# Attention and two quantised convolutions on one core: ScalarE and VectorE in the order of the source, and a Winograd combination in three pieces

## The chip, the cores and the metric

The kernel runs on one core of a Trainium2 chip. The metric is the device time of one execution in microseconds, the median of the runs. The engines are TensorE (PE, matmul), VectorE (DVE), ScalarE (ACT), GpSimd (POOL) and SyncE (SP, which issues DMAs).

## The reference

The input x has 16 images of 128 channels by 32 x 32 pixels, float32. Two layers follow each other:

```
# layer 0: attention over the 1024 pixels of each image, 4 heads of 128 channels
q, k, v = split(w_qkv . x + b_qkv)
out = softmax(q k^T / sqrt(128)) v           # per image and head
x1 = w_out . out + b_out + x
# layer 1: two 3x3 convolutions with 4-bit activations and weights, batch norms
a = round(clip(x1, 0, 1) * 15) / 15
y = batchnorm(conv3x3(a, quantised(w1)))
z = batchnorm(conv3x3(round(clip(y, 0, 1) * 15) / 15, quantised(w2)))
result = z + x1
```

The batch norms take mean and variance over all 16 images, so the second convolution can't begin before the first one is done for the last image.

## The kernel before

**Steps.** The work lies in `fast_path`. The attention has 64 heads (16 images x 4); each but the last takes NK = 4 steps, k = 0 to 3, and the last one has a form of its own (`score_unit`, `attend_unit`). A step does, in the order of the source:

1. `scores(g, k)`: four score products on TensorE into `pss` (512 wide, pool `ps_s`, three PSUM buffers), each followed by an exponential on ScalarE (L556) into a slice of the tile `e` (pool with two buffers). VectorE then makes the combinations that a Strassen-like product needs: T3 (L559), T1 and T2 (L560), T4 (L563), and adds the row sums into `es` (L567 at k=1, which reads the `e` of k=0 and of k=1; L569 at k=2 and 3).
2. `run(step, 0)`: what the table `later` holds for the first half of the step.
3. `attend(g, k-1)`: seven products of `e` and `vo` into the four banks `psa` (one buffer each). The last product of a head (k=3) goes to bank 0.
4. `run(step, 1)`: what `later` holds for the second half.

**What `later` holds.** The loop over heads fills it with `at(step, half, function)`; entries of one key keep the order in which they were added, and head g's are added before head g+1's. For a head that ends at step `end`: `sum_up` 0 (row sums, `part`, L630) at `end`, first half; `evacuate` (four copies of `psa` to SBUF on ScalarE, L600) at `end`, second half; `combine` 0, 1, 2 (L610 to L623: copies on ScalarE, adds on VectorE) at `end`+1 to `end`+3; `sum_up` 1 to 3 (L649 to L662); `normalise` (L679 to L694) at `end`+3, second half, whose last operation releases the image. `project_u` for the next head and `project_v` for the next image (vo, L535 to L538) lie between these.

**The first convolution** is spread over the attention too. After every second image (an image pair p) its inputs are quantised (`quantize`, L260 to L262) at `end`+5, and a Winograd form of the convolution runs in small pieces through the next six heads: `six_columns` (L827 to L842) and `six_rows` (L853) on VectorE, `six_products` (psw on TensorE, a copy on ScalarE at L862, then VectorE at L884 to L904), in three parts s = 0, 1, 2. `first_statistics` ends the pair at `end`+24. Image 14 has a smaller form (`products`), the last image a plain convolution.

**What sets the order.** On TensorE every product is chained to the one before it (`product` with `tc.issue_after`), so that it keeps the order of the source. `tc.issue_after(ins)` lets what is traced within it come after `ins` on its engine, with no wait added. ScalarE and VectorE have no such chain in the attention: the planner orders their instructions, by the order of the source among those that are ready by its own estimates of time. SyncE issues the writes of x1 (L696) and of the finished first-convolution outputs of eight images (L955); ScalarE's queue issues the loads of x (L423), each of which needs the buffer of an image two earlier.

The lines that set the order of the evacuation and of attend's last product:

```
for to, ps in zip(evs[g], psa.pop(g)):          # evacuate, banks 0, 1, 2, 3
    nc.scalar.copy(to, ps)
...
if k % 2:                                       # attend, (bank, half, value, exponential)
    seven = [seven[i] for i in (1, 0, 3, 2, 5, 4)] + [(0, 1, S3, T3)]
```

Of the kernel before, what the change touches and what calls it, by code (L numbers as in the profile page):

```python
# [192 lines left out]
def fast_path(  # L193
# [29 lines left out]

    outer = ExitStack()
# [28 lines left out]
    def quantize(b, src, scale, bias, r0=0, r1=H):  # L253

        cut = slice(r0 * W, r1 * W)
        t = qtp.tile([P, (r1 - r0) * W], F32, tag="qt", name="qt")
        if b == B - 1 and scale == A_LEVELS and r1 == H:
            nc.vector.tensor_scalar(t, src[:, cut], scale, 0.0, ALU.mult, ALU.max)
        else:
            nc.scalar.activation(t, src[:, cut], AF.Relu, bias=bias, scale=scale)  # L260
        nc.vector.tensor_scalar(t, t, A_LEVELS, MAGIC, ALU.min, ALU.add)
        return nc.vector.tensor_scalar(  # L262
            pads[b % NPAD][:, r0 + 1 : r1 + 1, 1 : W + 1],
            t.rearrange("p (h w) -> p h w", w=W),
            MAGIC,
            None,
            ALU.subtract,
        )
# [82 lines left out]
    def sums_range(b):  # L351
        flat = sums[:, b * NH : (b + 1) * NH, :].rearrange("p g k -> p (g k)")
        nc.vector.tensor_reduce(ext[:, 0, b : b + 1], flat, AX.X, ALU.min)
        nc.vector.tensor_reduce(ext[:, 1, b : b + 1], flat, AX.X, ALU.max)
# [23 lines left out]
    with ExitStack() as ph:  # L378
# [86 lines left out]
        def fold_a(h):  # L465
# [10 lines left out]
            nc.vector.tensor_scalar(at_sb[:, h, :], ps[:, 0:P], qscale, None, ALU.mult)  # L476
            nc.vector.tensor_scalar(au_sb[:, h : h + 1], bias, qscale, None, ALU.mult)

        def fold_b():
# [3 lines left out]
            nc.scalar.copy(bt_sb[:, 1, 1:], ps)  # L483
            nc.vector.tensor_copy(bt_sb[:, 1, 0], ps[:, NH - 1])
            nc.scalar.copy(bt_sb[:, 0, :, TOP], bt_sb[:, 1, :, TOP])  # L485
            nc.vector.tensor_tensor(
                bt_sb[:, 0, 0:NH, BOTTOM], bt_sb[:, 1, 0:NH, BOTTOM], bt_sb[:, 1, 0:NH, TOP], ALU.subtract
            )
            nc.vector.tensor_copy(bt_sb[:, 0, NH, BOTTOM], bt_sb[:, 1, NH, BOTTOM])

        def fold_bo():
# [9 lines left out]
            nc.vector.tensor_tensor(bo2_sb, ps, bo_sb, ALU.add)  # L501

        def project_u(g, hf, ps=None):
# [7 lines left out]
            if g == 0 and hf == 0:  # L511
                nc.vector.tensor_scalar(dst, ps, au_sb[:, h : h + 1], None, ALU.add)
            else:
                copied = nc.scalar.activation(dst, ps, AF.Identity, bias=au_sb[:, h : h + 1])  # L514
                if g == 0:
                    load_rest(copied.ins)
# [8 lines left out]
        def project_v(b, k, c, ps=None):  # L525
# [9 lines left out]
            nc.scalar.copy(v[:, c : c + 3 : 2], ps.rearrange("p (h a o) -> p a h o", a=2, o=PH))  # L535
            if c == 1:
                nc.vector.tensor_tensor(v[:, S2], v[:, S3], v[:, A22], ALU.subtract)
                nc.vector.tensor_tensor(  # L538
# [9 lines left out]
        def scores(g, k, between=None):  # L548
# [4 lines left out]
            for i, (c, m) in enumerate(((0, 1), (1, 1), (0, 0), (1, 0))):  # L553
                ps = ps_s.tile([P, HALF], F32, tag="s", name=f"pss_{g}_{k}_{i}")
                score(ps, b, g, k + NK * c, ts(m, HALF))
                exps[:] = [nc.scalar.activation(e[:, 2 * c + 1 - m], ps, AF.Exp).ins]  # L556
                if between and i in between:
                    between[i]()
            nc.vector.tensor_tensor(e[:, T3], e[:, B12], e[:, B22], ALU.add)  # L559
            nc.vector.tensor_tensor(  # L560
                e[:, T1 : T2 + 1 : T2 - T1], e[:, B12 : B11 + 1], e[:, B11 : T3 + 1 : T3 - B11], ALU.subtract
            )
            nc.vector.tensor_tensor(e[:, T4], e[:, T2], e[:, B21], ALU.add)  # L563
            mine = e[:, T4 : T3 + 1]
            if k == 1:
                sides[g] = esp.tile([P, NHF, HALF], F32, tag="es", name=f"es_{g}")
                nc.vector.tensor_tensor(sides[g], es[g, 0][:, T4 : T3 + 1], mine, ALU.add)  # L567
            elif k > 1:
                added = nc.vector.tensor_tensor(sides[g], sides[g], mine, ALU.add)  # L569
                sums_added[:] = [added.ins]  # L570
# [26 lines left out]
        def evacuate(g):  # L597
            evs[g] = [evp.tile([P, HALF], F32, tag=f"s{i}", name=f"ev_{g}_{i}") for i in range(4)]
            for to, ps in zip(evs[g], psa.pop(g)):
                nc.scalar.copy(to, ps)  # L600
# [5 lines left out]
        def combine(g, part):  # L606
            sa, sb, s3, sd = evs[g]
            if part == 0:
                y = avs[g, "y"] = evp.tile([P, HALF], F32, tag="y", name=f"y_{g}")
                nc.scalar.copy(y[TOP], s3[BOTTOM])  # L610
                nc.scalar.copy(y[BOTTOM], sd[TOP])  # L611
                nc.scalar.copy(sd[TOP], sd[BOTTOM])
                nc.vector.tensor_tensor(y, sa, y, ALU.add)  # L613
                return
            y = avs[g, "y"]
            if part == 1:
                nc.scalar.copy(s3[BOTTOM], y[TOP])
                nc.vector.tensor_tensor(y, y, s3, ALU.add)
            elif part == 2:
                nc.scalar.copy(sa[BOTTOM], y[BOTTOM])  # L620
                avs[g] = avp.tile([P, N], F32, tag="av", name=f"av_{g}")
                nc.vector.tensor_tensor(avs[g][:, HALF:], y, sd, ALU.add)
                nc.vector.tensor_tensor(avs[g][:, 0:HALF], sa, sb, ALU.add)  # L623
                evs.pop(g), avs.pop((g, "y"))

        def quadrant_sums(total):
# [3 lines left out]
            nc.vector.tensor_reduce(  # L630
# [8 lines left out]
        def sum_up(g, part):  # L639
# [5 lines left out]
            elif part == 1:  # L645

                side = smp.tile([Q, P // Q, n], F32, tag="side", name=f"side_{g}")
                for a in range(P // Q):
                    nc.scalar.copy(side[:, a, :], sides[g][ts(a, Q), :])  # L649
                sides[g] = side  # L650
            elif part == 2:
                total = smp.tile([Q, n], F32, tag="total", name=f"total_{g}")
                nc.vector.tensor_reduce(
# [4 lines left out]
                nc.vector.tensor_tensor(first, first, second, ALU.add)  # L658
                nc.vector.reciprocal(rinv[0:Q, :], total)
            else:  # L660
                for a in range(1, P // Q):
                    nc.scalar.copy(rinv[ts(a, Q), :], rinv[0:Q, :])  # L662

        def last_sums(part, cut):
# [7 lines left out]
            nc.vector.reciprocal(rinv, ps)  # L672

        def spread(g, cut):
# [4 lines left out]
            nc.vector.transpose(rb, rinv.unsqueeze(2).to_broadcast([P, rinv.shape[1], Q]))  # L679
            return rb  # L680

        def normalise(g):
# [3 lines left out]
            if h == 0:  # L686
                accs[b] = accp.tile([P, N], F32, tag="acc", name=f"acc_{b}")
                nc.vector.tensor_tensor(accs[b], av, rb, ALU.mult)
                return
            nc.vector.tensor_tensor(av, av, rb, ALU.mult)  # L690
            nc.vector.tensor_tensor(accs[b], accs[b], av, ALU.add)
            if h == NH - 1 or g == LAST - 1:

                nc.vector.scalar_tensor_tensor(accs[b], accs[b], bo2_sb, xt[b], ALU.add, ALU.add)  # L694
# [15 lines left out]
        def score_unit(u):  # L710
# [9 lines left out]
            exps[:] = [nc.scalar.activation(e, ps, AF.Exp).ins]  # L720

        def attend_unit(u):
# [8 lines left out]
            elif u == FIRST_UNIT[i] + 1:  # L731
# [6 lines left out]
                nc.vector.tensor_tensor(totals[i], units[(u - 1) // 4][:, (u - 1) % 4], e, ALU.add)  # L738
            else:
                nc.vector.tensor_tensor(total, total, e, ALU.add)  # L740
# [15 lines left out]
            elif u + 1 == FIRST_UNIT[i + 1]:  # L756
# [3 lines left out]
                nc.scalar.copy(avs[LAST, i], psa[LAST, i])  # L760
                sides[LAST, i] = quadrant_sums(total)

        def normalise_group(i):
# [5 lines left out]
            nc.vector.tensor_tensor(rb, avs.pop((LAST, i)), rb, ALU.mult)  # L769
            nc.vector.tensor_tensor(x1[:, cut], x1[:, cut], rb, ALU.add)  # L770
# [14 lines left out]
        def transform_weights():  # L785
            with tc.issue_after(sums_added[0]):
                by_row = once.tile([P, 4, 3, P], BF16, tag="rows", name="wino_rows")
                w = wq[0].rearrange("p (y x) o -> p y x o", x=3)
                nc.vector.tensor_copy(by_row[:, 0], w[:, 0])
                nc.vector.tensor_copy(by_row[:, 1], w[:, 2])  # L790
                nc.vector.tensor_tensor(by_row[:, 3], w[:, 0], w[:, 2], ALU.add)
                nc.vector.tensor_tensor(by_row[:, 2], by_row[:, 3], w[:, 1], ALU.add)
                nc.vector.tensor_tensor(by_row[:, 3], by_row[:, 3], w[:, 1], ALU.subtract)
                nc.vector.tensor_scalar(by_row[:, 2:4], by_row[:, 2:4], 0.5, None, ALU.mult)
                left, mid, right = [by_row[:, :, x, :] for x in range(3)]
                nc.vector.tensor_copy(wino[:, 0], left)
                nc.vector.tensor_copy(wino[:, 5], right)
                nc.vector.tensor_tensor(wino[:, 4], left, right, ALU.add)
                nc.vector.tensor_tensor(wino[:, 1], wino[:, 4], mid, ALU.add)
                nc.vector.tensor_tensor(wino[:, 2], wino[:, 4], mid, ALU.subtract)  # L800
                nc.vector.scalar_tensor_tensor(wino[:, 4], right, 4.0, left, ALU.mult, ALU.add)
                nc.vector.scalar_tensor_tensor(wino[:, 3], mid, 2.0, wino[:, 4], ALU.mult, ALU.add)
                nc.vector.scalar_tensor_tensor(wino[:, 4], mid, -2.0, wino[:, 4], ALU.mult, ALU.add)
                flat = wq[0].rearrange("p t o -> p (t o)")
                nc.vector.tensor_scalar(flat, flat, FIRST, None, ALU.mult)
# [11 lines left out]
        def six_columns(p, s, g):  # L817
# [8 lines left out]
            if s == 0:  # L826
                nc.vector.tensor_tensor(t, at(1), at(2), add)  # L827
                nc.vector.tensor_tensor(u, at(3), at(4), add)
                nc.vector.scalar_tensor_tensor(one, t, -4.0, u, mult, add)
                nc.vector.tensor_tensor(t, at(1), at(2), sub)  # L830
                nc.vector.tensor_tensor(u, at(4), at(3), sub)
                nc.vector.scalar_tensor_tensor(two, t, 4.0, u, mult, add)
            elif s == 1:
                nc.vector.tensor_tensor(t, at(3), at(1), sub)
                nc.vector.tensor_tensor(u, at(4), at(2), sub)
                nc.vector.scalar_tensor_tensor(one, t, 2.0, u, mult, add)
                nc.vector.scalar_tensor_tensor(two, t, -2.0, u, mult, add)
            else:
                nc.vector.scalar_tensor_tensor(t, at(2), -5.0, at(4), mult, add)
                nc.vector.scalar_tensor_tensor(one, at(0), 4.0, t, mult, add)  # L840
                nc.vector.scalar_tensor_tensor(u, at(3), -5.0, at(5), mult, add)
                nc.vector.scalar_tensor_tensor(two, at(1), 4.0, u, mult, add)  # L842

        def six_rows(p, s, i):
# [6 lines left out]
            for k, (x, y, op) in enumerate(OF_FOUR):  # L851
                into = tiles[p][:, i, k].rearrange("p (g i j) -> p g i j", g=2, j=D4)
                nc.vector.tensor_tensor(into, pick(x), pick(y), op)  # L853

        def two_products(name, weights, operands, scale, k):
# [6 lines left out]
            nc.scalar.mul(ms[name][:, k : k + 2], ps, scale)  # L862
# [5 lines left out]
        def six_products(p, s, i, k):  # L868
# [15 lines left out]
            nc.vector.tensor_tensor(e, two, of(2).unsqueeze(1).to_broadcast(list(two.shape)), ALU.add)  # L884
            nc.vector.tensor_tensor(e[:, 0], e[:, 0], of(3), ALU.add)
            nc.vector.tensor_tensor(e[:, 1], e[:, 1], of(3), ALU.subtract)
# [6 lines left out]
            if s == 2:  # L893
                y = y[3 * i]
                nc.vector.tensor_tensor(y, y, other if i else one, ALU.add)
# [629 lines left out]
```

## Time and profile before

| what | value |
|---|---|
| runs | 2093.58 and 2095.42 us, median 2094.5 |
| the profiled execution | 2096.73 us |
| its span | 2094.9 us, granted TensorE clock 0.987 |
| TensorE busy (matmul) | 2014.9 us, 96% |
| VectorE busy | 1796.4 us, 86% |
| ScalarE busy | 1278.9 us, 61% |
| GpSimd busy | 19.6 us, 1% |

The span runs from the first to the last instruction. In the lines of the profile, a group or an instruction is named by line, engine, operation, output and input; a number in square brackets with an arrow is the idle time of the engine just before it and what ended that. In the timeline the first two columns are start and duration in microseconds, and x4 means four instructions merged into one row. Ends of matmuls are modelled. The attention fills the time to about 2000 us; the second convolution and the end take the rest.

### The profile page before, as it was taken

What the parts mean: (1) busy time and instruction counts of PE and PEld (TensorE: products, weight loads), DVE (VectorE), ACT (ScalarE), POOL (GpSimd) and SP (SyncE); (2) the same over time, 40 slices, a digit from 0 to 9 for tenths busy, and PEclk for the clock granted to TensorE, in tenths of its full rate; (3) what the DMA queues carried; (4) which work ended last, traced back from release to release, by engine and by line L of the source; (5) the groups of instructions that cost most, each with busy time, mean ns of one, the idle gap of its engine ahead of it and who ended that gap; (6) DMA issues with size and microseconds to landing.
All of it is one profiled execution on the core that took longest, in us unless ns stands there. A gap on an engine that the chain in (4) does not pass through costs nothing.

```text
span 2094.9 us, 25194 instructions
## 1 busy us (share of the span) xinstructions
PE 2014.9 (96%) x9505; PEld 890.8 (43%) x9505; DVE 1796.4 (86%) x2692; ACT 1278.9 (61%) x2480; POOL 19.6 (1%) x29
## 2 busy tenths in 40 slices
PE   8999999999999999999999999999999999999994
PEld 3443434443353434534345343444345343453452
DVE  4878788897988988898888988989789888889998
ACT  4565566566566666656656656656665665665575
POOL 0000000000000000000000000000000000000020
PEclk9999999999999999999999999999999999999997
DMA  1000000000000000000000000000000000000064
GB/s 40 23 1 21 1 21 1 20 1 1 21 1 21 1 21 1 1 21 1 21 1 20 21 1 20 1 21 21 1 21 1 21 21 21 1 1 11 21 251 162
DMA packets 13329, 45.86 MB, mean 22 GB/s; under 512 B 1424, under 2 KB 1808, under 8 KB 13200
## 3 DMA queue, kind: packets, MB, share of 16 engines
q1 hardware_dynamic: 10000, 34.15, 4.3%
q10 hardware_dynamic: 3200, 10.03, 1.5%
q8 instruction: 76, 1.25, 0.2%
q14 instruction: 53, 0.43, 0.1%
HBM read 23.21 MB, written 20.97 MB: 21 GB/s over the span
## 4 chain that ended last, share of the span: by engine, by line
PE 64%; DVE 24%; ACT 8%; issue 3%; DMA 0%; POOL 0%; DVEq 0%; ACTq 0%
PE pss L408 27%; PE psa L408 26%; DVE e L560 4%; PE psv L408 4%; PE psu L408 4%; ACT e L556 3%; DVE es L569 2%; DVE e L563 2%; ACT ev L600 2%; DVE part L630 2%; DVE e L559 1%; DVE es L567 1%; PE psc L287 1%; ACT side L649 1%; DVE av L690 1%
## 5 line engine op out<-in xcount | busy, mean ns | idle before, releaser
L408 PE MATMUL pss<-u,x 128*64 128x512 f32 (+1 forms) x4128 | 1061.0, 592 | 25.8 <-ACT e L556 23.2
L408 PE MATMUL psa<-e,vo 128*64 128x512 f32 (+1 forms) x3624 | 934.6, 595 | 19.3 <-DVE e L563 19.3
L556 ACT ACTIVATE e<-pss 128x512 f32<-128x512 f32 x1008 | 579.9, 594 | 308.3 <-PE pss L408 258.6
L408 PEld LDWEIGHTS pss<-u,x 128*64 128x64 f32 x4128 | 405.5, 137 | 500.6 <-issue 343.1
L408 PEld LDWEIGHTS psa<-e,vo 128*64 128x64 f32 x3624 | 363.4, 138 | 463.7 <-issue 375.0
L560 DVE TENSOR_TENSOR e<-e 128x1024 f32<-128x1024 f32 x252 | 307.2, 1219 | 26.3 <-ACT e L556 23.7
L559 DVE TENSOR_TENSOR e<-e 128x512 f32<-128x512 f32 x252 | 172.2, 683 | 86.0 <-ACT e L556 85.3
L563 DVE TENSOR_TENSOR e<-e 128x512 f32<-128x512 f32 x252 | 172.4, 684 | 10.1 <-DVE e L560 0.9
L408 PE MATMUL psv<-bt_sb,x 128*64 128x512 f32 x512 | 179.7, 593 | 1.0 <-ACT bt_sb L485 1.0
L408 PE MATMUL psu<-x,at_sb 128*64 128x512 f32 x512 | 174.7, 604 | 2.3 <-ACT wino L862 1.5
L649 ACT COPY side<-part 32x32 f32<-32x32 f32 x252 | 54.5, 216 | 179.1 <-DVE part L630 176.6
L600 ACT COPY ev<-psa 128x512 f32<-128x512 f32 x252 | 137.9, 586 | 42.3 <-PE psa L408 40.4
L569 DVE TENSOR_TENSOR es<-es,e 128x1024 f32<-128x1024 f32 x126 | 153.8, 1220 | 1.9
L535 ACT COPY vo<-psv 128x512 f32<-128x512 f32 x128 | 75.0, 586 | 80.8 <-PE psv L408 80.7
L514 ACT ACTIVATE u<-psu,au_sb 128x512 f32<-128x512 f32 x127 | 87.3, 687 | 22.7 <-PE psu L408 21.0
L862 ACT ACTIVATE wino<-psw 128x512 f32<-128x512 f32 x92 | 55.0, 598 | 70.5 <-PE psw L408 69.3
L679 DVE STREAM_TRANSPOSE rb<-sums 128x1024 f32<-128x1024 f32 (+1 forms) x66 | 79.6, 1207 | 12.0 <-ACT sums L662 11.9
L613 DVE TENSOR_TENSOR y<-ev,y 128x512 f32<-128x512 f32 x63 | 43.3, 688 | 52.8 <-ACT y L611 52.8
L408 PEld LDWEIGHTS psv<-bt_sb,x 128*64 128x64 f32 x512 | 58.7, 137 | 61.3 <-issue 49.2
L408 PEld LDWEIGHTS psu<-x,at_sb 128*64 128x64 f32 x512 | 54.4, 139 | 65.8 <-issue 52.4
L630 DVE TRANSPOSE_TENSOR_REDUCE part<-es 128x32 f32<-128x1024 f32 (+1 forms) x65 | 79.6, 1224 | 0.6
L567 DVE TENSOR_TENSOR es<-e,e 128x1024 f32<-128x1024 f32 x63 | 76.8, 1219 | 0.3
(198 smaller groups left out, 1435.4 us busy)
## 6 DMA issues: line engine op xcount, KB each, us to landing
x_dram<-acc SPq DMA_DIRECT2D x16, 512.0 KB, 4.3
x<-in_x_dram ACTq DMA_DIRECT2D x15, 512.0 KB, 4.6
res<-x_dram SPq DMA_DIRECT2D x1, 7680.0 KB, 32.4
y_dram<-y SPq DMA_DIRECT2D x4, 1024.0 KB, 4.0
back<-y_dram SPq DMA_DIRECT2D x1, 4096.0 KB, 14.1
out_dram<-back SPq DMA_DIRECT2D x8, 512.0 KB, 4.3
out_dram<-y SPq DMA_DIRECT2D x9, 256.0 KB, 2.4
out_dram<-y SPq DMA_DIRECT2D x3, 512.0 KB, 5.0
```

The lines of the kernel that those rows point to most:

```text
L408: done = nc.tensor.matmul(out_, lhsT=lhsT, rhs=rhs, start=start, stop=stop)
L514: copied = nc.scalar.activation(dst, ps, AF.Identity, bias=au_sb[:, h : h + 1])
L556: exps[:] = [nc.scalar.activation(e[:, 2 * c + 1 - m], ps, AF.Exp).ins]
L559: nc.vector.tensor_tensor(e[:, T3], e[:, B12], e[:, B22], ALU.add)
L560: nc.vector.tensor_tensor(e[:, T1 : T2 + 1 : T2 - T1], e[:, B12 : B11 + 1], e[:, B11 : T3 + 1 : T3 - B11], ALU.subtract)
L563: nc.vector.tensor_tensor(e[:, T4], e[:, T2], e[:, B21], ALU.add)
L567: nc.vector.tensor_tensor(sides[g], es[g, 0][:, T4 : T3 + 1], mine, ALU.add)
L569: added = nc.vector.tensor_tensor(sides[g], sides[g], mine, ALU.add)
L600: nc.scalar.copy(to, ps)
L630: nc.vector.tensor_reduce(part, total.rearrange("p (k c) -> p k c", c=Q), AX.X, ALU.add, apply_transpose=True,)
L649: nc.scalar.copy(side[:, a, :], sides[g][ts(a, Q), :])
L679: nc.vector.transpose(rb, rinv.unsqueeze(2).to_broadcast([P, rinv.shape[1], Q]))
```

## The change

A small class hands every call to an engine and chains it behind the last instruction that it handed out. Through it go all ScalarE and VectorE computations of the attention and of the first convolution within it: `quantize`, `sums_range`, `fold_a`, `fold_b`, `fold_bo`, `project_u`, `project_v`, `scores`, `evacuate`, `combine`, `sum_up`, `last_sums`, `spread`, `normalise`, `score_unit`, `attend_unit`, `normalise_group`, `transform_weights`, the Winograd functions. Not through it go the DMAs that ScalarE issues, `conv_weights`, `constants`, `bn_constants`, `statistics`, `gather`, the plain convolutions and all that follows the attention.

The second edit takes four operations on the pair's outputs (L901 to L904) out of `six_products` (where they ran with the last piece of part s=1, at `end`+18, second half) and makes of them a function `six_mix`, called in two halves at `end`+20.

```diff
+    class InOrder:
+        def __init__(self, engine):
+            self.engine, self.last = engine, None
+        def __getattr__(self, name):
+            def call(*args, **kwargs):
+                with tc.issue_after(self.last) if self.last else nullcontext():
+                    done = getattr(self.engine, name)(*args, **kwargs)
+                self.last = done.ins
+                return done
+            return call
+
+    act, vec = InOrder(nc.scalar), InOrder(nc.vector)
...
             for to, ps in zip(evs[g], psa.pop(g)):
-                nc.scalar.copy(to, ps)
+                act.copy(to, ps)
...
             elif i == 1:
                 sums, differences = (y[0], y[1]) if s == 0 else (y[2], y[3])
-                nc.vector.tensor_tensor(sums, one, other, ALU.add)
-                nc.vector.tensor_tensor(differences, one, other, ALU.subtract)
-                if s == 1:
-                    nc.vector.tensor_tensor(y[0], y[0], y[2], ALU.add)
-                    nc.vector.scalar_tensor_tensor(y[2], y[2], 3.0, y[0], ALU.mult, ALU.add)
-                    nc.vector.scalar_tensor_tensor(y[1], y[3], 2.0, y[1], ALU.mult, ALU.add)
-                    nc.vector.scalar_tensor_tensor(y[3], y[3], 6.0, y[1], ALU.mult, ALU.add)
+                vec.tensor_tensor(sums, one, other, ALU.add)
+                vec.tensor_tensor(differences, one, other, ALU.subtract)
+
+        def six_mix(p, n):
+            y = [
+                y2[p].rearrange("p g (i j c) -> p (g i) j c", j=D4, c=4)[..., c] for c in (n, n + 2)
+            ]
+            if n == 0:
+                vec.tensor_tensor(y[0], y[0], y[1], ALU.add)
+                vec.scalar_tensor_tensor(y[1], y[1], 3.0, y[0], ALU.mult, ALU.add)
+            else:
+                vec.scalar_tensor_tensor(y[0], y[1], 2.0, y[0], ALU.mult, ALU.add)
+                vec.scalar_tensor_tensor(y[1], y[1], 6.0, y[0], ALU.mult, ALU.add)
...
+                    for n in range(2):
+                        at(end + 20, n, six_mix, p, n)
                     at(end + 24, 0, first_statistics, b)
```

## The prediction

> **What bounds the kernel now.** I read the page first, then the matrix multiplies' gaps in the timeline, then the chain behind those gaps, then the lists of waits.
>
> ```profile
> PE 2014.9 (96%) x9505; PEld 890.8 (43%) x9505; DVE 1796.4 (86%) x2692; ACT 1278.9 (61%) x2480; POOL 19.6 (1%) x29
> ...
> PE   8999999999999999999999999999999999999994
> ```
>
> TensorE is nearly full in every slice, so the change can gain only what its gaps hold. An image pair of the attention (32 steps) recurs every 247.2 us: the x_dram writes of every second image start at 1026.16, 1273.89 and 1521.11 us. In such a pair TensorE shows these gaps over 0.25 us (timeline of PE, cut at the gaps):
>
> ```profile
> 1410.24 4.71 PE L408 MATMUL psa<-e,vo 128*64 128x512 f32 x13 [2.71 <-DVE e L563]
> ...
> 1426.24 1.08 PE L408 MATMUL pss<-u,x 128*64 128x512 f32 x4 [0.55 <-ACT e L556]
> ...
> 1468.55 1.08 PE L408 MATMUL pss<-u,x 128*64 128x512 f32 x4 [0.30 <-ACT e L556]
> ...
> 1539.39 1.08 PE L408 MATMUL pss<-u,x 128*64 128x512 f32 x4 [1.60 <-ACT e L556]
> ```
>
> That is 5.2 us per pair. The same list from 98 us to 1954 us sums to 42 us, 2% of the time. The 2.71 is the combination of the pair: six y operations run on VectorE in a block, and the exponentials' sums wait behind it (timeline of DVE, one pair later):
>
> ```profile
> 1648.58 1.10 DVE L898 TENSOR_TENSOR y<-six 128x512 f32<-128x512 f32 x1
> 1649.52 1.11 DVE L899 TENSOR_TENSOR y<-six 128x512 f32<-128x512 f32 x1
> 1650.46 1.15 DVE L901 TENSOR_TENSOR y<-y 128x512 f32<-128x512 f32 x1
> ...
> 1654.56 0.67 DVE L559 TENSOR_TENSOR e<-e 128x512 f32<-128x512 f32 x1
> ```
>
> The planner does not keep the source order today. ScalarE starts evacuating a finished head before its last product is done, because the banks finish one by one:
>
> ```profile
> 1225.03 0.58 ACT L600 COPY ev<-psa 128x512 f32<-128x512 f32 x1
> 1225.87 0.58 ACT L600 COPY ev<-psa 128x512 f32<-128x512 f32 x1 [0.26 <-PE psa L408]
> 1226.73 1.07 ACT L600 COPY ev<-psa 128x512 f32<-128x512 f32 x2 [0.27 <-PE psa L408]
> ```
>
> The head's last psa matmul starts only at 1226.10 and ends at 1226.69. The same trace also shows what happens when all four copies come late and in one block (ACT, then PE):
>
> ```profile
> 1289.57 2.05 ACT L600 COPY ev<-psa 128x512 f32<-128x512 f32 x4
> 1291.48 0.64 ACT L556 ACTIVATE e<-pss 128x512 f32<-128x512 f32 x1
> ```
> ```profile
> 1292.18 1.08 PE L408 MATMUL pss<-u,x 128*64 128x512 f32 x4 [1.61 <-ACT e L556]
> ```
>
> The first exponential of the next step is delayed, and the fourth score, which needs that PSUM buffer (ps_s has three), starts 0.06 us after it ends.
>
> Last, the step that has no filler on VectorE shows what the order of the source costs there:
>
> ```profile
> 1308.23 1.23 DVE L560 TENSOR_TENSOR e<-e 128x1024 f32<-128x1024 f32 x1 [0.17 <-ACT e L556]
> 1309.56 0.69 DVE L563 TENSOR_TENSOR e<-e 128x512 f32<-128x512 f32 x1
> 1310.29 1.23 DVE L569 TENSOR_TENSOR es<-es,e 128x1024 f32<-128x1024 f32 x1
> 1311.55 1.25 DVE L630 TRANSPOSE_TENSOR_REDUCE part<-es 128x32 f32<-128x1024 f32 x1
> ```
>
> An operation that reads its predecessor's result starts 1.33 us (1024 wide) or 0.73 us (512 wide) after it. Independent neighbours follow after 1.14 and 0.60 us (1650.46 after 1649.52 is likewise 0.94 for 1.11). Today the planner puts independent work between the dependent ones.
>
> **The Trainium skill.** "PSUM — Partial Sum Buffer", section Engine vs sequencer instructions: ScalarE's and VectorE's queues are strict FIFO and matmuls complete in program order. The trace agrees: at 1289.57 exponentials stand behind copies. "Perfetto Trace Analysis", section Optimizing Tensor Performance: independent groups rotate through banks so that one's evacuation overlaps the next one's matmuls; at 1225.03 it does. "VectorE: DVE Perf Modes", section The DRAIN you can't avoid: the next operation waits until the pipe is empty. The trace shows this only for dependent neighbours; independent ones overlap by 0.08 us, and I use the trace.
>
> **Part 1: the pair's combination in pieces.** Four operations of about 1.02 us move from step 18 after the pair's end to steps 20 (two, half 0) and 20 (two, half 1). No operation is added and no DMA moves; SP's and POOL's queues are not passed. The two sums and differences (L898, L899) stay. This frees the 2.7 us gap, 7 times, but puts 4.4 us (dependent order) into step 20, where the old image's last normalisation already lags.
>
> **Part 2: ScalarE in source order.** evacuate copies the banks in the order 0, 1, 2, 3, and bank 0 gets the head's very last product (k=3 is odd: S3, T3). So none of the four can start before the end of the last product. Let E be the time at which TensorE can issue the next matmul. The last matmul ends at about E+0.38, the first copy starts at E+0.42, copies follow each other by 0.48 (1289.57 to 1291.48 for four), the exponential starts at E+2.34 and ends at E+2.92, and the fourth score starts at E+2.98. Three scores cover 3 x 0.86 = 2.58. The stall is 0.40 us at a plain head. Where a value projection comes ahead of the copies in the list (head 0 of each image), the copies wait for its psv: stall 0.88. Where a psw product comes ahead (steps 8 and 20): 0.68. Where the projection follows the copies (head 3): its 0.86 us of matmuls hide it. A pair has two of 0.88, 0.68, 0.40 and 0 each: 3.9 us. Seven pairs give 27, and the first 8 heads (no psw) 2.5: 30 us. Behind the waiting copy stand the exponentials, and TensorE waits for these.
>
> **Part 3: VectorE in source order.** I tally its work per step against TensorE's length. A step is 16 score and 14 attend matmuls at 0.215 = 6.45 us, plus 0.86 for each u or v projection, 0.43 for a psw, all stretched by 1.2% (clock 0.987). VectorE's e operations in order: 0.73+1.33+0.73+1.14 = 3.93 (2.66 at k=0, which has no es). To this come, in dependent order: part 1.15 (k=0); y 0.6 (k=1); y and total 1.55 (k=2); two av adds 1.2 and normalise 2.44, 3.7 or 5.04 (k=3; heads 0, 1-2, 3); vo 1.1; quantize 1.3; six_columns 2.35, 1.5 or 1.6 per image; six_rows 0.85; six_products with k=2 1.4, plus 1.98 or 1.1 for y. The exponentials alone hold es to 6.96 us after a step's start. The sums that matter (steps after the pair's end; us from the step's start):
>
> ```
> step  PE    queue free  es done  all done   lag into next
>  3    6.5      1.1        7.0      13.2        6.7
>  5    7.8      4.4        8.3      12.5        4.7
>  7    7.0      6.0       10.0      14.4        7.5
>  8    7.4      7.5       10.1      15.7        8.3
>  9    8.5      8.3       12.2      16.2        7.7
> 12    8.3      8.5       11.2      16.7        8.4
> 13    7.8      8.4       12.3      12.9        5.1
> 19    6.5      4.1        8.0      16.0        9.4
> 20    7.0      9.4       12.1      18.0       11.1
> 21    8.6     11.1       15.0      19.4       10.8
> ```
>
> Most of the lag is hidden: e is needed a step later, after the next scores. The tight place is k=1. There es (L567) is the last reader of the e buffer of k=0 (the pool has two), and the next step's exponentials need this buffer; the fourth score needs the first of them. Stall = es done + 0.7 - (step + 2.6): step 9 1.8 us, step 13 2.5, step 21 4.5, steps 20 to 25 another 1.1. Together 9.9 us per pair, 69 for seven. In the trace of before this wait exists ("ACT e L556 <- DVE es L567", 25.9 us in 30 times, longest 1.8), but it never reached TensorE for long.
>
> This tally is sensitive: with all VectorE work 5% shorter it gives 3.6 us per pair, with 10% 1.6, with 5% more 17. The trace has no stage in strict order to fix it; below nothing is excluded, since lag absorbs all. I take the middle.
>
> **Sum.** Against the profiled execution (2096.7 us; its span 2094.9, 1.8 around it): +30 + 69 - 38 (the gaps listed, less the last two near 1951, which belong to the last images) = +61, so 2157.7. The runs' median is 2.2 lower: 2155.5, say 2156. The stage after the attention is not touched except through the first convolution's quantize: 0.
>
> **The rivals.**
> - A: only the copies cost. VectorE's lag stays inside the buffers because the work is some 10% less than tallied. Speaks for it: VectorE has 14% idle. Against: dependent neighbours lose their overlap 96 times a pair in the e operations alone. 30 + 11 - 38 = +3: 2098.
> - B, not slower: the order itself pays. Today bulk work is put ahead of e operations by wrong due times; in source order e comes first and all gaps over 0.25 us go. The place is the head change: it decides if the copies are done early enough that the first exponential ends within 2.58 us of E, for which the first copy would have to start before E+0.02. For: the 2.71 gap is such a mistake. Against: bank 0 is last. -38: 2057.
> - C: on top of the forecast, the load of x (L423) is not in the chain, and is queued on ScalarE by the planner's times. At step 20 its releaser (L694) ends near 9.4 us, while the copies could go at 7.4: 2 us on seven pairs, +14: 2170.
>
> **How the numbers follow.** Forecast 0.60, A 0.18, B 0.10, C 0.12. The range runs from A (2098, a little below it) to the tally with 5% more work and C's part, 2094.5 + 17 x 7 + 30 - 38 + 14 = 2220: 2096 to 2222. The same sum with 5% less work gives 2112. Two per cent, about what a measurement of this kernel can tell from no change, is 42 us: slower means above 2136. Of the forecast some five sixths lie above (0.50), nearly all of C (0.11): slower 0.61. B reaches faster only if the smaller gaps go as well: 0.03. Same 0.36.
>
> **What would show it.** In the profile of after, the copies at L600 should come as x4 of about 2.0 us after the last psa, PE gaps of 0.4 to 0.9 "<-ACT e L556" at head changes, a long gap near step 21 with "ACT e L556 <- DVE es L567" far above 25.9 us, and no 2.7 us psa gap near step 18. "ACT side L649 <- DVE part L630" (176.6 us today) should shrink, as side copies stand behind exponentials. Wrong: if L567 stays below 30 us in total (then A), or if the copies still start before the head's last product ends (then the part on ScalarE falls), or if psa waits on L563 grow most (then the e buffers are not the tight place).

## The result and the profile after

The changed kernel takes 2179.5 us (2178.4 to 2180.6) against 2094.5 us before: a ratio of 1.041, interval 1.036 to 1.045. The forecast was 2156 in 2096 to 2222. The profiled execution's span is 2176.6 us, 81.7 more than before, at a granted clock of 0.979. All chained instructions now carry the line of the helper, L233, and TensorE's products L425, so the page is read by tiles.

The page's busy line and TensorE's slices:

```profile
PE 2041.7 (94%) x9505; PEld 857.9 (39%) x9505; DVE 1856.0 (85%) x2692; ACT 1286.5 (59%) x2480; POOL 20.3 (1%) x29
...
PE   9999998999998999999999999999999899998984
```

No engine became the bound over the whole span: VectorE's busy time grows by 60 us at the same count of instructions, but its share falls by a point. The time lies in TensorE's gaps. One image pair of the timeline of PE, cut at gaps over 0.25 us (as before, the last bracket is idle time and its releaser):

```profile
1301.30 1.08 PE L425 MATMUL pss<-u,x 128*64 128x512 f32 x4 [0.56 <-ACT e L233]
1330.64 1.08 PE L425 MATMUL pss<-u,x 128*64 128x512 f32 x4 [0.36 <-ACT e L233]
1359.64 1.08 PE L425 MATMUL pss<-u,x 128*64 128x512 f32 x4 [0.56 <-ACT e L233]
1370.34 1.97 PE L425 MATMUL pss<-u,x 128*64 128x512 f32 x4 [2.54 <-ACT e L233]
1403.79 1.08 PE L425 MATMUL pss<-u,x 128*64 128x512 f32 x4 [0.99 <-ACT e L233]
1429.45 1.08 PE L425 MATMUL pss<-u,x 128*64 128x512 f32 x4 [0.56 <-ACT e L233]
1459.44 1.08 PE L425 MATMUL pss<-u,x 128*64 128x512 f32 x4 [0.56 <-ACT e L233]
1472.53 1.92 PE L425 MATMUL pss<-u,x 128*64 128x512 f32 x4 [4.75 <-ACT e L233]
```

Eight gaps with 10.9 us stand where four with 5.2 us stood; the 2.71 before a psa product is gone. The five short ones are head changes. Here ScalarE copies a head's four banks in one block after its last product (timeline of ACT, the gap of 0.36):

```profile
1327.59 0.35 ACTq L440 DMA_DIRECT2D x<-in_x_dram  x1
1328.04 2.05 ACT L233 COPY ev<-psa 128x512 f32<-128x512 f32 x4 [2.72 <-PE psa L425]
1329.95 1.62 ACT L233 ACTIVATE e<-pss 128x512 f32<-128x512 f32 x3
```

At this head change the load of x, which is not in the chain, stands ahead of the copies: it is issued when `acc` is done (1327.55), and the copies start 0.33 us after the end of the last product (1327.71). At the four gaps of 0.56 us it is another ScalarE instruction that stands ahead of the copies, a copy of psv to vo (twice) or of psw (twice), and waits for its own product.

The three long gaps are another wait. The largest, in the timelines of DVE, then ACT:

```profile
1461.84 1.12 DVE L233 TENSOR_TENSOR y<-y 128x512 f32<-128x512 f32 x1
1462.99 1.15 DVE L233 SCALAR_TENSOR_TENSOR y<-y 128x512 f32<-128x512 f32 x1
1464.03 1.25 DVE L233 TRANSPOSE_TENSOR_REDUCE part<-es 128x32 f32<-128x1024 f32 x1
1465.19 2.24 DVE L233 SCALAR_TENSOR_TENSOR y<-y 128x512 f32<-128x512 f32 x2
1467.34 0.47 DVE L233 TENSOR_REDUCE ext<-sums 128x1 f32<-128x128 f32 x2
1467.72 2.81 DVE L233 TENSOR_TENSOR e<-e 128x512 f32<-128x512 f32 x3
1470.56 1.22 DVE L233 TENSOR_TENSOR es<-e,e 128x1024 f32<-128x1024 f32 x1
```
```profile
1471.88 1.57 ACT L233 ACTIVATE e<-pss 128x512 f32<-128x512 f32 x3 [5.25 <-DVE es L233]
```

Step 20's bulk work (y, part, ext: 5.9 us) runs first, then the three combinations of step 21's e, then es, the last reader of the e buffer that step 22's first exponential needs. The exponential starts 0.10 us after es ends, and the fourth score 0.65 us after that. The list of waits sums it up (us in total, times, longest):

```profile
ACT e L233 <- DVE es L233: 90.5, 29, 5.3
PE pss L425 <- ACT e L233: 86.8, 61, 4.8
```

The first was 25.9 us in 30 times and reached TensorE little; the second was 23.2.

### The profile page after: what moved, and what is told of

Same layout as the page of the kernel before. It is cut to its first block, busy times and chain, and to the rows that moved or that the text cites. A ratio compares the mean times of both kernels' runs of the same rounds, so it can differ in the third digit from the quotient of the medians.

```text
span 2176.6 us, 25201 instructions
## 1 busy us (share of the span) xinstructions
PE 2041.7 (94%) x9505; PEld 857.9 (39%) x9505; DVE 1856.0 (85%) x2692; ACT 1286.5 (59%) x2480; POOL 20.3 (1%) x29
## 4 chain that ended last, share of the span: by engine, by line
PE 56%; DVE 34%; ACT 7%; issue 2%; DMA 0%; DVEq 0%; POOL 0%; ACTq 0%; POOLq 0%
PE pss L425 23%; PE psa L425 22%; DVE e L233 10%; PE psv L425 5%; PE psu L425 4%; DVE es L233 4%; DVE work L233 4%; ACT ev L233 3%; DVE y L233 3%; DVE av L233 2%; DVE acc L233 2%; ACT e L233 2%; DVE rb L233 2%; DVE part L233 2%; DVE six L233 1%
## 5 line engine op out<-in xcount | busy, mean ns | idle before, releaser
L425 PE MATMUL pss<-u,x 128*64 128x512 f32 (+1 forms) x4128 | 1079.9, 598 | 89.0 <-ACT e L233 86.8
L425 PE MATMUL psa<-e,vo 128*64 128x512 f32 (+1 forms) x3624 | 927.2, 591 | 6.0 <-ACT e L233 3.7
L233 ACT ACTIVATE e<-pss 128x512 f32<-128x512 f32 x1024 | 593.9, 607 | 434.6 <-PE pss L425 344.0
L233 DVE TENSOR_TENSOR e<-e 128x512 f32<-128x512 f32 x756 | 656.0, 868 | 222.2 <-ACT e L233 176.0
L425 PEld LDWEIGHTS pss<-u,x 128*64 128x64 f32 x4128 | 392.3, 138 | 590.9 <-issue 402.2
L425 PEld LDWEIGHTS psa<-e,vo 128*64 128x64 f32 x3624 | 345.6, 139 | 473.4 <-issue 449.1
L425 PE MATMUL psv<-bt_sb,x 128*64 128x512 f32 x512 | 190.3, 594 | 0.5 <-DVE bt_sb L233 0.5
L233 ACT COPY ev<-psa 128x512 f32<-128x512 f32 x252 | 129.4, 605 | 86.8 <-PE psa L425 70.0
L233 ACT COPY vo<-psv 128x512 f32<-128x512 f32 x128 | 75.6, 591 | 173.0 <-PE psv L425 172.7
L425 PE MATMUL psu<-x,at_sb 128*64 128x512 f32 x512 | 166.8, 640 | 1.4 <-ACT wino L233 1.0
L233 DVE TENSOR_TENSOR es<-es,e 128x1024 f32<-128x1024 f32 (+1 forms) x134 | 159.8, 1192 | 4.5
L233 ACT ACTIVATE wino<-psw 128x512 f32<-128x512 f32 x92 | 54.8, 596 | 112.6 <-PE psw L425 112.6
L233 DVE TENSOR_TENSOR vo<-vo 128x256 f32<-128x256 f32 (+1 forms) x128 | 71.2, 557 | 46.6 <-ACT vo L233 44.4
L233 ACT ACTIVATE u<-psu,au_sb 128x512 f32<-128x512 f32 x127 | 87.3, 688 | 10.8 <-PE psu L425 8.4
L425 PEld LDWEIGHTS psv<-bt_sb,x 128*64 128x64 f32 x512 | 60.5, 137 | 57.9 <-issue 54.8
L233 ACT COPY ev<-y 64x512 f32<-64x512 f32 x126 | 77.7, 616 | 5.7 <-DVE y L233 2.9
L425 PEld LDWEIGHTS psu<-x,at_sb 128*64 128x64 f32 x512 | 49.5, 147 | 76.7 <-issue 74.1
L233 ACT COPY y<-ev 64x512 f32<-64x512 f32 x126 | 77.8, 618 | 3.1
L233 DVE STREAM_TRANSPOSE rb<-sums 128x1024 f32<-128x1024 f32 (+1 forms) x66 | 79.6, 1206 | 0.1
L233 DVE TRANSPOSE_TENSOR_REDUCE part<-es 128x32 f32<-128x1024 f32 (+1 forms) x65 | 79.3, 1220 | 0.1
L233 DVE TENSOR_TENSOR es<-e,e 128x1024 f32<-128x1024 f32 x63 | 77.1, 1224 | 2.1
L425 PE MATMUL psw<-tiles,wino 128*64 128x256 bf16 x368 | 61.6, 273 | 1.2 <-DVE tiles L233 1.2
## 6 DMA issues: line engine op xcount, KB each, us to landing
res<-x_dram SPq DMA_DIRECT2D x1, 7680.0 KB, 32.3
out_dram<-y SPq DMA_DIRECT2D x9, 256.0 KB, 2.4
```

What stands on the lines that cost most here:

```text
L233: done = getattr(self.engine, name)(*args, **kwargs)
L425: done = nc.tensor.matmul(out_, lhsT=lhsT, rhs=rhs, start=start, stop=stop)
```

## The experiments

Differences are to the kernel after, unless said; ratios are to the kernel before, with their intervals.

### The pieces alone: mix_only

The kernel before, with only the combination moved to `six_mix` at `end`+20; no chain.

> The kernel before with only the combination in pieces; both engines are left to the planner. Theory (the long y block of step 18 makes the 2.7 us psa gap of each pair): seven gaps of 2.7 us and their pipeline tails go, nothing else moves, 2072 to 2080 us. Rival (the pieces at step 20 collide with the end of the image and only move the gap): 2092 to 2100 us.

2074.1 us, 0.990 (0.988 to 0.992). The second edit by itself gains 20.4 us. The 2.71 us wait of psa is gone, but a gap of 1.34 us is new, and the 0.55 has become 0.80 (timeline of PE):

```profile
1401.98 1.08 PE L408 MATMUL pss<-u,x 128*64 128x512 f32 x4 [1.34 <-ACT e L556]
...
1410.93 1.08 PE L408 MATMUL pss<-u,x 128*64 128x512 f32 x4 [0.80 <-ACT e L556]
...
1453.25 1.08 PE L408 MATMUL pss<-u,x 128*64 128x512 f32 x4 [0.31 <-ACT e L556]
...
1524.10 1.08 PE L408 MATMUL pss<-u,x 128*64 128x512 f32 x4 [1.61 <-ACT e L556]
```

That the gain is near seven times 2.7 us is partly chance: TensorE's gaps over the attention (those over 0.25 us, from 30 us on) fall by only 10.3 us (44.3 to 34.0), and I estimate that some 8.6 us come from a higher clock, of which more below. This is the fastest version of all; the slowdown is due to the order.

### One engine in order: vec_only, act_only

```diff
-    act, vec = InOrder(nc.scalar), InOrder(nc.vector)
+    act, vec = nc.scalar, InOrder(nc.vector)        # vec_only
+    act, vec = InOrder(nc.scalar), nc.vector        # act_only
```

> The changed kernel with ScalarE left to the planner; VectorE keeps the order of the source. Theory (two separate costs: late copies on ScalarE, lag on VectorE that meets the last reader of e): the short gaps at head changes go, the long ones at steps 9 and 21 stay, 2140 to 2160 us. Rival (all of the loss is VectorE's order, the copies' order is free): as the changed kernel, 2172 to 2185 us.

> The changed kernel with VectorE left to the planner; ScalarE keeps the order of the source. Theory: short gaps of 0.4 to 0.6 us at five head changes of a pair, no long ones, 2100 to 2125 us. Rival (ScalarE's order is free): near 2076 us. Rival (ScalarE's order is the greater cost, because each of its instructions waits for VectorE): over 2140 us.

vec_only 2171.7 us, 1.037 (1.035 to 1.039); act_only 2099.5 us, 1.002 (1.001 to 1.003). Over mix_only, VectorE's order costs 98 us, ScalarE's 25, both 105. The costs don't add: under VectorE's order ScalarE's adds only 8 by the medians, and the intervals of the two ratios overlap. The timeline of PE of vec_only shows why:

```profile
1366.14 1.98 PE L425 MATMUL pss<-u,x 128*64 128x512 f32 x4 [4.09 <-ACT e L573]
1399.64 1.08 PE L425 MATMUL pss<-u,x 128*64 128x512 f32 x4 [1.60 <-ACT e L573]
...
1467.57 1.67 PE L425 MATMUL pss<-u,x 128*64 128x512 f32 x4 [5.02 <-ACT e L573]
```

Without the 0.56 us stalls of the copies the long gaps are longer (4.09 for 2.54, 1.60 for 0.99, 5.02 for 4.75), and over the attention the gaps sum to the same (98.3 us, 98.2 after). VectorE's queue paces these stretches: what TensorE saves ahead of them, it waits for in them. The vec_only forecast (2140 to 2160) failed because it subtracted the copies at full price.

act_only came out just under its theory's range, and not by that theory alone: four gaps of 0.56 us stand in a pair, but a long one too, at step 22 (timelines of PE and ACT):

```profile
1420.21 1.97 PE L425 MATMUL pss<-u,x 128*64 128x512 f32 x4 [2.64 <-ACT e L233]
```
```profile
1419.56 1.57 ACT L233 ACTIVATE e<-pss 128x512 f32<-128x512 f32 x3 [3.15 <-DVE es L584]
```

So the wait for es does not need VectorE's order: with the pieces at step 20 and ScalarE in order it is there too, at about half the length. Its 25 us are thus not the price of the copies alone.

### The banks in another order: banks

`evacuate` copies banks 1, 3, 2, 0 instead of 0, 1, 2, 3.

> The changed kernel with one edit: the four copies of a finished head take the banks in the order in which the last step of attend finishes them (1, 3, 2, 0) instead of 0, 1, 2, 3. Theory: three copies run before the last product ends, the first exponential of the next step comes 1.4 us earlier, the five short gaps of a pair go: 4 to 5 us per pair, 2145 to 2155 us. Rival (the copies' place is hidden by lag elsewhere): 2172 to 2182 us.

2177.1 us, 1.039 (1.037 to 1.041): the theory fell. One reason is plain in its ACT timeline, and should have been seen beforehand, as the prediction has these cases in its sum:

```profile
1422.99 0.59 ACT L233 COPY vo<-psv 128x512 f32<-128x512 f32 x1 [3.66 <-PE psv L425]
1423.47 2.06 ACT L233 COPY ev<-psa 128x512 f32<-128x512 f32 x4
```

At this head change, where a 0.56 us gap stays, a vo copy stands ahead of the ev copies, so it is psv that sets their start, and no order of banks helps. The other three gaps of 0.56 us stay in the same way, behind a vo copy or a copy of psw. Only the gap of 0.36 goes, and there the load of x also moved behind the copies, so this run does not tell what the order of the banks is worth. And where something was saved, the long waits took it: step 10's gap grew to 2.97, step 14's to 1.63.

### Another reader of the e buffer: es_copy

At k=0 VectorE copies T4 and T3 into `es` at once; at k=1 it adds in place. The buffer of k=0 is then free before k=1's combinations.

> The changed kernel with one edit: at k=0 VectorE copies T4 and T3 into es at once (one more 1024 wide operation per head, after part), and at k=1 adds in place, so that the e buffer of k=0 is free without the sum of k=1. Theory (the last reader of this buffer is what the exponentials of steps 10 and 22 wait for): the gaps of 2.5 and 4.7 us shrink to below 1.5 us, 2105 to 2150 us, although VectorE has more work. Rival (VectorE as a whole is too late, and the next thing it owes is missed instead): psa then waits for T4 for as long, 2170 to 2200 us.

2159.2 us, 1.031 (1.029 to 1.033): 20 us gained, in the expectation's gap between theory and rival. The 2.54 and 4.75 us waits are gone; these stand in their place (timeline of PE):

```profile
1366.98 0.50 PE L425 MATMUL psw<-tiles,wino 128*64 128x256 bf16 x4 [2.40 <-DVE tiles L233]
...
1458.88 3.65 PE L425 MATMUL psa<-e,vo 128*64 128x512 f32 x14 [2.71 <-DVE e L233]
```

So the e buffer was the tight place, but behind it VectorE owed the next things almost as late. TensorE's gaps over the attention fall from 98.2 to 84.3 us; a part of the gain is the clock, whose loss (worked out under `fill`) falls from 32.3 to 11.9 us.

### Dependent neighbours or bulk work: no_dep, no_mix

```diff
-  e[:, T1 : T2 + 1 : T2 - T1], e[:, B12 : B11 + 1], e[:, B11 : T3 + 1 : T3 - B11], ALU.subtract
+  e[:, T1 : T2 + 1 : T2 - T1], e[:, B12 : B11 + 1], e[:, B11 : B21 + 1 : B21 - B11], ALU.subtract
-  vec.tensor_tensor(e[:, T4], e[:, T2], e[:, B21], ALU.add)      # no_dep
+  vec.tensor_tensor(e[:, T4], e[:, B22], e[:, B21], ALU.add)
-                    for n in range(2):                           # no_mix
-                        at(end + 20, n, six_mix, p, n)
```

> The changed kernel with the inputs of two of VectorE's e operations replaced, sizes and counts kept: T2 is made from B11 and B21 instead of B11 and T3, T4 from B22 and B21 instead of T2 and B21, so that neither reads its predecessor's result (the attention's values are other ones for it). Theory (a good part of the lag is that dependent neighbours do not overlap): some 0.3 us per step less on VectorE, step 21 meets the e buffer 2 us or more earlier, the 4.7 us gap falls below 3 us, 2140 to 2165 us. Rival (the lag is bulk work standing ahead of the e operations, the dependence is small): the gap stays over 4 us, 2172 to 2180 us.

2179.2 us, 1.040 (1.038 to 1.042): nothing (timeline of DVE, the same place as above):

```profile
1467.21 2.60 DVE L233 TENSOR_TENSOR e<-e 128x512 f32<-128x512 f32 x3
```

2.60 for 2.81 us, 0.2 us per step; the gap there goes from 4.75 to 4.52. Step 10's gap falls more, from 2.54 to 1.49, but step 14's grows from 0.99 to 1.95, and the 0.36 at the head change with the load of x to 1.03. VectorE is busy 22 us less in all, and no time is gained.

The edit loosens less than it was meant to. Of the three operations only the last now starts before its predecessor ends (by 0.08 us). The second still starts 0.1 us after the first: it writes T1 over B12, which the first one reads, and I take this for the reason. And es still reads T4. So one dependence of three was taken away, at 0.2 us a step; what all three cost stays open.

> Left out: the four combining operations of the image pair (both halves), so the outputs of the first convolution are not combined; all else as in the kernel after. Theory: what makes the sums of the exponentials late at step 21 of a pair is the bulk work that the order of the source puts ahead of them, above all these four operations (about 4.5 us of VectorE at step 20). Without them the 4.75 us gap should fall under 1 us and the low clock after it should go, so each of seven pairs gains 4 to 7 us: 2130 to 2150. Rival: the lag is taken up by the next owed thing (a psa product that waits for T4, or step 22's own bulk), the gap only moves, and the gain is below 2 us per pair: 2165 to 2180.

2146.1 us, 1.025 (1.023 to 1.027): 33 us gained, as the theory had it. The gap at step 22 (timeline of PE):

```profile
1449.16 1.08 PE L425 MATMUL pss<-u,x 128*64 128x512 f32 x4 [0.38 <-ACT e L233]
```

Taking 4.5 us of bulk work away cut 4.4 us off the gap. It is bulk work standing ahead of the exponentials' combinations that makes them late. Step 10's gap, which has other bulk ahead of it, stays at 2.56. The clock's loss falls too, from 32.3 to 11.9 us. This run takes the work away altogether; `order_only`, next, keeps it and changes its place alone.

### The pieces under the order: order_only

The four operations go back to `end`+18, in one block; both engines stay in order.

> The changed kernel with the four combining operations back at step 18, second half, both engines still in the order of the source. Theory (in strict order VectorE owes the same work before step 21 wherever the four stand): the long gap near step 21 stays and psa waits at step 20 come in addition, 2178 to 2200 us. Rival (the pieces themselves at step 20 make the 4.7 us gap): the gap goes, 2150 to 2165 us.

2171.3 us, 1.037 (1.036 to 1.039), which neither expectation had: 8 us faster than after by the medians. The two ratios' intervals overlap, but `tail` below, which differs from after by one relu and ran on the same chip as order_only, has 1.042 (1.040 to 1.044). So the move that gains 20 us without the order gains nothing with it and probably loses some 8. The sum of the gaps over the attention is the same (98.8 us, 98.2 after), but split differently: where after has 0.99 and 4.75, order_only has

```profile
1397.90 1.08 PE L425 MATMUL pss<-u,x 128*64 128x512 f32 x4 [2.77 <-ACT e L233]
...
1448.64 3.22 PE L425 MATMUL psa<-e,vo 128*64 128x512 f32 x13 [1.47 <-DVE e L233]
...
1460.44 4.08 PE L425 MATMUL psa<-e,vo 128*64 128x512 f32 x12 [2.01 <-DVE e L233]
```

The gap at step 22 is gone, so it is the place of these four operations that makes it; but they make others elsewhere. What order_only saves is clock: its loss over the attention is 13.7 us against 32.3, as the next experiment explains.

### The clock after a long gap: fill

Products that nobody reads stand before the fourth score of steps 10 and 22, 10 and 20 of them.

> The changed kernel with unread matmuls added on TensorE ahead of the fourth score of steps 10 (10 of them, about 2.2 us) and 22 (20, about 4.3 us) of each pair, where it stands idle 2.5 and 4.7 us. They write no result that is used. Theory (a long idle stretch itself is followed by a stretch at half clock, and this is a part of the loss beside the wait): the granted clock stays at 1.0 there, and the time falls by 10 to 22 us to 2157 to 2170, though 210 matmuls are added. Rival (the lower clock has another reason, or the added work costs what it fills): 2178 to 2195 us.

2172.4 us, 1.038 (1.036 to 1.039): 7 us gained, just short of the expectation. In windows of 2 us, after (columns: us, busy of PE, PEld, DVE, ACT, POOL with counts, the clock, DMA share, GB/s) shows

```profile
1472.00:1474.00 2.00, 1.47 (x4) 0.49 (x6) 1.97 (x4) 1.46 (x3) 0.00 (x0) 0.66 0.04 8
1474.00:1476.00 2.00, 2.00 (x8) 0.55 (x6) 1.93 (x4) 1.21 (x2) 0.00 (x0) 0.50 0.00 0
```

and fill, after its unread products,

```profile
1468.00:1470.00 2.00, 2.00 (x12) 0.69 (x10) 1.93 (x5) 1.75 (x4) 0.00 (x0) 1.00 0.00 0
```

Right after the 4.75 us gap the clock is 0.50, and TensorE's products start in pairs 0.85 us apart, where fill's are 0.43 us apart. Summed as (1 - clock) x 2 us over the attention, I estimate the loss as 32.3 us in after and 5.1 in fill; in after, 3.8 us of it lie within gaps, where TensorE had nothing to do. Yet only 7 us came back. Step 14's gap grew from 0.99 to 2.73, 12 us in seven pairs: as I read it, the slow stretch had also given VectorE time to catch up.

### Two that gained nothing: tail, mix_sides

In `tail` the last image's relu is taken out of ScalarE's chain. In `mix_sides`, mix_only's `side` copies (L649 there) must come after their head's psa copies.

> The changed kernel with the last image's relu on ScalarE (L277) left out of the chain, so that the last head's exponentials need not stand behind it. Theory (this relu waited 10.4 us for acc and TensorE 3.7 us behind it): 4 to 10 us less, 2169 to 2176 us. Rival (VectorE's own order delays the last head): no change within 2 us.

> The kernel before with the combination in pieces and one partial order: ScalarE's four copies of part (L649) of a head come after that head's four copies of psa. No other chain. Theory (the 1.6 us gap of each pair that is left comes from row-sum copies that the planner puts ahead of the psa copies while VectorE is late): it goes, 2055 to 2070 us. Rival (the row sums then come too late and the lag moves to normalise): 2074 to 2090 us.

tail: 2181.9 us, 2.4 over after, so its theory fell; a wait of TensorE of 5.34 us for `part` on VectorE takes the place of its 3.73 us behind ScalarE's 10.38 us for `acc`. mix_sides: 2129.9 us, 1.017 (1.015 to 1.018), 56 us slower than mix_only, far outside both expectations. The single edge went with another order of ScalarE's whole list. In its timeline of ACT small copies now wait for VectorE with the exponentials behind them:

```profile
1444.02 0.61 ACT L622 COPY ev<-y 64x512 f32<-64x512 f32 x1 [1.35 <-DVE y L620]
1444.66 0.60 ACT L556 ACTIVATE e<-pss 128x512 f32<-128x512 f32 x1
```
```profile
1445.31 1.28 PE L408 MATMUL pss<-u,x 128*64 128x512 f32 x4 [2.87 <-ACT e L556]
```

Its wait "ACT ev L622 <- DVE y L620" comes to 93.5 us in 59 times (24.4 in 24 in mix_only, at L620 and L618 there). Why the planner chose that order was not tried.

## Why the prediction was right, and where its sum was not

**Direction and places: right.** The copies come as x4 of 2.05 us after the last psa (at four of the five gaps behind one more copy), the 2.7 us gap is gone, "ACT e <- DVE es" went from 25.9 to 90.5 us, the long gap stands at step 21 to 22, and "ACT side <- DVE part" (176.6) has left the list. Rival A (this wait stays below 30 us) and rival B (all gaps go) fell. Rival C came, but small and at another place: once a pair, at the head change of the 0.36 us gap, the load of x stands ahead of the copies. The prediction has the first copy 0.04 us after the end of the last product; here it is 0.33, which is most of that gap. ScalarE's copies are also put down to `acc` five times (14.0 us), with no gap of TensorE over 0.1 us after them.

**The sum per pair.** A gap in the timeline understates a stall by the 0.38 us that the modelled end of the last product covers, as the prediction's E has it.

| per pair, us | predicted | measured |
|---|---|---|
| copies at head changes | 3.9 | 4.5 (five gaps, 2.6 shown + 5 x 0.38) |
| es late | 9.9 | 9.4 (2.54 + 0.99 + 4.75, + 3 x 0.38) |
| gaps of before | -5.4 | -6.7 (5.2 + 4 x 0.38) |
| lower clock after gaps, estimated | 0 | 2.3 (outside of gaps: (28.5 - 12.5) / 7) |
| sum | 8.4 | 9.5 |

ScalarE's u activations come near the sum: after minus before is 0.3 us at the 16th and 70.4 at the 127th, 6.9 pairs later: 10.1 per pair. The other 0.6 I leave open.

The sums per row are closer than their parts, which is luck. With the 0.38 us, steps 10, 14 and 22 stall for 2.9, 1.4 and 5.1 us where the prediction had 1.8, 2.5 and 4.5, and of its 1.1 us after step 22 nothing came; it had itself said that 5% less or more work on VectorE turns its 9.9 us into 3.6 or 17. Of the copies, the four heads with another copy ahead stall for 0.94 us, where the prediction had 0.88 twice and 0.68 twice. The plain head without the load of x comes out right: 0.07 us shown, 0.45 in all, for 0.40.

**What was mis-sized or missing.** The 23 us to the forecast are in the main two terms. First, 1.1 us per pair by the table and 1.7 by the u activations, 8 to 12 us in all: the sum left out the half-speed clock (2.3), and also left out the tails of before's gaps (1.3 the other way). Second, the end: from the last u activation to the end of the program another 11 us are lost (150.2 against 139.0), which the prediction put at 0 ("the stage after the attention is not touched"). In the last head ScalarE's chained relu stands ahead of the exponentials (timelines of ACT and PE):

```profile
2071.03 0.63 ACT L233 ACTIVATE qt<-acc 128x512 f32<-128x512 f32 x1 [10.38 <-DVE acc L233]
```
```profile
2072.19 1.08 PE L425 MATMUL psa<-e,vo 128*64 128x256 f32 x8 [3.73 <-ACT e L233]
```

It is not shown to be the cause: `tail` takes it out of the chain, and the end is no shorter (150.8 us). Either order alone lengthens this end, from 138.8 us in mix_only to 146.3 in act_only and 151.7 in vec_only. Which operations do it stays open.

**Right size, wrong weight on the cause.** Against rival A the prediction set the lost overlap of dependent neighbours ("96 times a pair"). Behind this stands the Trainium skill's page "VectorE: DVE Perf Modes", section The DRAIN you can't avoid, where the next operation waits for an empty pipe, and one that isn't held starts earlier; the traces have both, as independent neighbours overlap by 0.08 us and dependent ones do not. no_dep took away one dependence of three, shows 0.2 us per step for it and no gain in time; no_mix, with 33 us, shows that the bulk work ahead counts for more. The tally came out near since it counted the bulk as well.

**Terms that don't add.** The prediction added copies (+30) and lag (+69) as independent. One at a time over mix_only the two orders measure 25 and 98, together 105, each with its share of the end, and the 25 with a wait for es. Nor is the piece term (about -19) independent: -20 without the order, some +8 with it, where the gaps keep their sum and only the clock differs.

**Open.** The gaps, tails and clock of the whole span, after minus before, come to 84 us (55 + 14 + 15, the clock's loss counted outside of gaps) against 81.7 measured. The copies' term was never removed alone: banks did not do it, for the reasons above, and vec_only removes the whole order of ScalarE with it.

## What to carry to other kernels

In a strict queue, look at each step not for how much an engine has to do, but for what bulk stands ahead of the one operation that frees a buffer. Taking the bulk away gained 33 us here, freeing the buffer by an earlier reader 20; putting the bulk two steps earlier left the sum of the gaps as it was. When the computations of a queue are put in order, look at its DMA issues too: left out of the order, one stood ahead of the copies once a pair here (what ordering it gains was not tried). Stalls caused by different engines on the same loop are not a sum: freeing one lets TensorE reach the next sooner and wait there, so price a removal by what is owed next. Before adding an order by hand to a planned kernel, try the local edit alone: here it gains 1%, and the order costs 5% over it.

## What the runs showed of the hardware

A gap of TensorE can cost more than itself. In 13 profiled kernels, from 200 to 1950 us, and counting a clock loss of at least 0.5 us within 10 us after the gap: 0 of 50 gaps between 1.2 and 1.8 us (as shown) had one, 35 of 94 between 1.8 and 2.8, and 52 of 54 longer ones, with a mean of 1.9 us lost for these. The Trainium skill's page "TensorE: Matmul & The Clock Gate", section HAM oscillation — how this bites in real kernels, gives the rule of no idle gaps over about 3.4 us; here losses begin at 1.95 us shown, some 2.3 with the modelled tail.

Length does not decide alone. In the attention of all 13 traces a stretch at half clock lasts 3.41 us or twice that, and within a trace the stretches start whole multiples of 3.41 us apart. So, as I read it, a gap of 2 to 3 us costs something or not by where it falls on this grid; no run moved a gap along it on purpose. In before, the 2.71 us gap at 1410.24 has such a stretch (1409.9 to 1413.3), and the 2.70 us gap at 1657.43, the same place one pair later, has none. In order_only, whose pairs recur every 256.0 us, 75 times 3.41, the same gaps escape each time: those of 2.58 and 2.77 us in all seven pairs have no loss, the one of 2.01 us has it in six of seven.

The kernel before had seven such episodes too, six after its seven gaps of about 2.7 us and one, twice as long, after the gap of 2.47 us at 1951.17, so closing these gaps gained more than the gaps: mix_only's clock loss is 5.1 us against 13.7.
